# Where a 65 MB zero fill is issued, where the next layer's weights are prepared, and which pools wait tile by tile, in a kernel of a mixture-of-experts layer and a Mamba layer

## The chip, the cores and the metric

The kernel runs on one core of a Trainium2 chip. The metric is the device time of one execution in microseconds (us); lower is better. Times are medians of several executions. One further execution was recorded by the profiler; all durations and positions below are from that one, counted from the start of its span.

## What is computed

The input is an image batch of 32 x 128 channels x 56 x 56, so T = 100352 tokens of 128 channels. Layer 0 is a 7x7 depthwise convolution, a norm over channels, and a mixture of 8 experts with 2 experts per token and a fixed capacity:

```
x = dwconv7x7(input); x = layernorm(x) ; xf = x.reshape(T, C)
topv, topi = top_k(xf @ Wg, 2);  wts = softmax(topv)
order = argsort(-wts[:, 0])              # better tokens get slots first
cap = int(1.25 * T / 8)                  # 15680 slots per expert
slot = expert * cap + position, dropped where position >= cap
buf = zeros(8 * cap, C).at[slot].set(x)  # dispatch
y = gelu(buf @ W1) @ W2                  # per expert
input + x + layer_scale * (sum of y[slot] * gate)
```

Layer 1 works on that result: a 1x1 convolution, then a 3x3 depthwise branch with batch norm and SiLU beside a Mamba branch (norm, projections, causal convolution, a scan over 3136 tokens with 16 states), a 1x1 convolution over both, and a skip connection. Everything is in f32. All biases are inputs, and the weights of both layers are inputs too.

## The kernel before

The work runs in five stages, one after the other. All of it is written in a tile framework: a program (the scheduler) lists the instructions of each engine in an order that it finds by simulating them, taking a later instruction first where an earlier one is not ready, and sets the semaphores. On the chip each engine then works strictly in that order. Only layer 1 fixes its order by hand (`manual_schedule`, in `layer1`).

- **Convolution** (lines 95 to 269): 8 batches b of 4 images. `fill` (L145) loads an image into the single buffer `xt` and PE transposes it into one of two slots; `conv` multiplies 32 groups of 4 channels with banded matrices `toep`. For b = 0 these are built from `raw` windows of `taps_d`, which is written from the first 7 loads of the kernel (L138, L139), and stored to `toep_d`; later batches load them from there (L172). `norm` takes 7 columns of 112 tokens at a time: DVE statistics (L197, L199), ACT scaling to `xa` (L207, three buffers), POOL gain and bias (L210, L211), SP's store to `res_d` (L213), PE transposes and logits (L221, L225). `top2` (L241 on) picks the two experts per token. The last batch's 16 norms have no convolution beside them.
- **Zero fill** (L272 to L274): every slot of `buf_d` that no token takes must hold zeros and, as its token number, T. The 125440 rows of 130 words are written by 14 DMAs from one row `zero` per partition, (k p) order: row k of 112 partitions at a time, 520 bytes per run. They stand after the convolution in the program and wait for nothing but a memset at the start.
- **Routing** (L277 to L442): 24 steps of a bisection for each expert's threshold (each: DVE counts, ACT `sign` sums at L344, PE totals at L323), ranks by scans, and slot numbers turned to 128 partitions. No DMA. DVE is busy most of the time.
- **Dispatch** (L452 to L473): 56 tiles `xg` of 28 x 128 rows, three buffers for each of two picks, loaded by SP from `res_d` (L465), completed by two small DVE copies (L466, L467), and scattered by 1568 indirect DMAs of 128 rows that POOL issues (L469). The scatters write `buf_d`, so they wait for all zero fills.
- **Experts** (L478 to L564): 248 groups of up to 512 rows are loaded from `buf_d` (L552), go through PE, and are added back to `res_d` by 984 indirect DMAs of POOL (L518). The loads wait for all scatters.
- **Layer 1** (L567 on): first the weights are prepared (L570 to L709: some 30 small DMAs, products with gains, transposes), then `layer1` runs 3584 units of a scan in a hand-written order, in which POOL, DVE and ACT each have one step per unit. Its first work is `fetch` (L760, L762), whose `yg` reads `res_d`, and `moe_pe` (L770, L772).

A pool is a region of SBUF; a pool that is opened after another was closed may take the same bytes. As a rule the first instruction that writes such a region waits until everything in the overlapped pools is done. `column` (L89) puts one-word-per-partition vectors into the pool `const`, which stays open throughout, so its loads wait for nothing. All loads and stores except `toep_d<-toep` and the indirect ones are issued by SP, and its DMAs go to the 16 DMA engines in one queue.

Of the kernel before, what the change touches and what calls it, by code (L numbers as in the profile page):

```python
# [13 lines left out]
C = 128  # L14
RW = C + 2
# [7 lines left out]
KF = FF // 128  # L23
GT = 4
# [19 lines left out]
def tile_kernel(tc: tile.TileContext, a: dict, out: bass.AP):  # L44
# [12 lines left out]
    with (  # L57
# [8 lines left out]

        zero = const.tile([TT, 1, RW], F32, name="zero")
        nc.gpsimd.memset(zero, 0.0)
        nc.gpsimd.memset(zero[:, :, C + 1].bitcast(I32), T)
# [26 lines left out]
        routed = tc.tile_pool(name="route", bufs=1)  # L96
# [175 lines left out]
        buf_t = buf_d[: E * CAP].rearrange("(k p) c -> p k c", p=TT)  # L272
        for k in range(0, E * CAP // TT, 80):
            nc.sync.dma_start(out=buf_t[:, k : k + 80, :], in_=zero.to_broadcast([TT, 80, RW]))  # L274


        with (  # L277
            tc.tile_pool(name="rt", bufs=1) as rt,
            tc.tile_pool(name="rs", bufs=2) as rs,
            tc.tile_pool(name="rp", bufs=2, space=PSUM) as rp,  # L280
        ):
            ones_tt = rt.tile([TT, TT], F32, name="ones_tt")
# [161 lines left out]


# [5 lines left out]
        with tc.tile_pool(name="dispc", bufs=1) as dc, tc.tile_pool(name="disp", bufs=3) as dp:  # L451
# [8 lines left out]
            for q in range(QB):  # L460
                for p0 in range(0, TT, XT):
                    for k in range(2):
# [5 lines left out]
                        for j in range(XT):  # L468
                            apart(nc.gpsimd.indirect_dma_start(  # L469
                                out=buf_d[:, :],  # L470
                                out_offset=bass.IndirectOffsetOnAxis(ap=slots[k][:, q, p0 + j : p0 + j + 1], axis=0),
                                in_=xg[:, j, :], in_offset=None,
                            ), "scatter")  # L473

# [3 lines left out]
        with (  # L478
            tc.tile_pool(name="ew", bufs=2) as ew,
            tc.tile_pool(name="eb", bufs=3) as eb,  # L480
# [86 lines left out]
        with (  # L567
            tc.tile_pool(name="w3", bufs=1) as wp,
            tc.tile_pool(name="p3", bufs=2, space=PSUM) as pmm,
        ):  # L570
            def mm_tile(name):
                return pmm.tile([128, 512], F32, name=name, tag="mm")

            def load(v, shape, name, pool=wp):
                t = pool.tile(shape, F32, name=name)
                nc.sync.dma_start(out=t, in_=v)
                return t

            def halves(v, name, pool=wp):
                return load(v.rearrange("(h p) -> p h", p=128), [128, 2], name, pool)  # L580

            cv1t = load(a["cv1_wT"], [C, C], "cv1t")
            cv1b = column(a["L1_conv_cv1_b"], "cv1b")
            def turned(v, t):

                for h in range(2):
                    nc.sync.dma_start(
                        out=t[h * HD : (h + 1) * HD],
                        in_=v[h * 128 : (h + 1) * 128].rearrange("(r d) k -> d r k", r=2),
                    )  # L590

            xpt = wp.tile([128, 2, XR], F32, name="xpt")
            turned(a["x_proj_wT"], xpt)
            dtt = load(a["dt_proj_wT"], [DR, DI], "dtt")
            cvlt = load(a["cv2_wT"][:C, :], [C, C], "cvlt")
            cv2b = column(a["L1_conv_cv2_b"], "cv2b")
            c1b3 = wp.tile([128, 2, 1], F32, name="c1b")
            turned(a["L1_conv_conv1d_b"].unsqueeze(1), c1b3)
            c1b = c1b3[:, :, 0]
            dtb = halves(a["L1_conv_dt_proj_b"], "dtb")  # L600


            aneg = wp.tile([128, 2, DS], F32, name="aneg")
            turned(a["L1_conv_A_log"], aneg)
            nc.scalar.activation(aneg, aneg, AF.Exp)
            nc.vector.tensor_scalar(aneg, aneg, 1e-25, -1.0, ALU.max, ALU.mult)


            bsc = column(a["L1_conv_bn_v"], "bsc")
            bbi = column(a["L1_conv_bn_m"], "bbi")  # L610
            bng = column(a["L1_conv_bn_g"], "bng")
            bnb = column(a["L1_conv_bn_b"], "bnb")
            nc.scalar.activation(bsc, bsc, AF.Sqrt, bias=eps5)
            nc.vector.reciprocal(bsc, bsc)
            nc.vector.tensor_tensor(bsc, bsc, bng, ALU.mult)
            nc.vector.tensor_tensor(bbi, bbi, bsc, ALU.mult)
            nc.vector.tensor_tensor(bbi, bnb, bbi, ALU.subtract)


            bnt = wp.tile([128, 2, 2], F32, name="bnt")  # L620
            for k in range(2):
                for r in range(2):
                    for j, v in enumerate((bbi, bsc)):
                        nc.scalar.copy(bnt[k * HD : (k + 1) * HD, r, j : j + 1], v[r * HD : (r + 1) * HD, :])

            wk = wp.tile([C, DC, DI], F32, name="wk")
            wz = wp.tile([C, DI], F32, name="wz")
            wo = wp.tile([128, 2, C], F32, name="wo")
            dd = wp.tile([128, 2, 128], F32, name="dd")
            dwd = wp.tile([C, 9, C], F32, name="dwd1")  # L630
            cv1c = wp.tile([C, C], F32, name="cv1c")
            cv1cb = wp.tile([C, 1], F32, name="cv1cb")
            zb = wp.tile([128, 2], F32, name="zb")
            early = wp.tile([DC - 1, DI], F32, name="early")
            with tc.tile_pool(name="w3t", bufs=1) as wt:
                dw1 = load(a["L1_conv_dw_w"].rearrange("c o h w -> c (o h w)"), [C, 9], "dw1", wt)
                for t in range(9):
                    nc.vector.tensor_scalar_mul(dwd[:, t, :], ident, dw1[:, t : t + 1])
                dcol = wt.tile([128, 2, 1], F32, name="dcol")
                turned(a["L1_conv_D"].unsqueeze(1), dcol)  # L640
                for h in range(2):
                    nc.vector.tensor_scalar_mul(dd[:, h, :], ident, dcol[:, h, :])


                row = wt.tile([C, 1], F32, name="row")
                nc.vector.tensor_reduce(row, cv1t, AX.X, ALU.add)
                nc.vector.tensor_scalar_mul(row, row, -1.0 / C)
                nc.vector.tensor_scalar(cv1c, cv1t, row, None, ALU.add)
                p = mm_tile("p_mb")
                nc.tensor.matmul(p[:, 0:1], lhsT=mean_w, rhs=cv1b, start=True, stop=True)  # L650
                nc.vector.tensor_tensor(cv1cb, cv1b, p[:, 0:1], ALU.subtract)

                gb = wt.tile([128, 2, C], F32, name="gb")
                nc.sync.dma_start(out=gb[:, 0, :], in_=a["L1_conv_ln_g"].partition_broadcast(128))
                nc.sync.dma_start(out=gb[:, 1, :], in_=a["L1_conv_ln_b"].partition_broadcast(128))
                inp = wt.tile([128, 4, C], F32, name="inp")
                turned(a["L1_conv_in_proj_w"][:DI], inp[:, 0:2, :])
                nc.sync.dma_start(  # L660
                    out=inp[:, 2:4, :], in_=a["L1_conv_in_proj_w"][DI:].rearrange("(h p) c -> p h c", p=128)
                )
                junk = wt.tile([128, 4, C], F32, name="junk")
                wb = wt.tile([128, 4], F32, name="wb")
                nc.vector.tensor_tensor(junk, inp, gb[:, 1:2, :].to_broadcast([128, 4, C]), ALU.mult)
                nc.vector.tensor_reduce(wb, junk, AX.X, ALU.add)
                nc.vector.tensor_tensor(inp, inp, gb[:, 0:1, :].to_broadcast([128, 4, C]), ALU.mult)
                wm = wt.tile([128, 4], F32, name="wm")
                nc.vector.tensor_reduce(wm, inp, AX.X, ALU.add)
                nc.vector.tensor_scalar_mul(wm, wm, 1.0 / C)  # L670
                nc.vector.tensor_tensor(inp, inp, wm.unsqueeze(2).to_broadcast([128, 4, C]), ALU.subtract)
                nc.vector.tensor_copy(zb, wb[:, 2:4])
                c1w = wt.tile([128, 2, DC], F32, name="c1w")
                turned(a["L1_conv_conv1d_w"].rearrange("i o k -> i (o k)"), c1w)

                miss = wt.tile([128, 2, DC], F32, name="miss")
                nc.vector.tensor_tensor(miss, c1w, wb[:, 0:2].unsqueeze(2).to_broadcast([128, 2, DC]), ALU.mult)
                for k in range(1, DC):
                    nc.vector.tensor_tensor(miss[:, :, k], miss[:, :, k], miss[:, :, k - 1], ALU.add)
                nc.vector.tensor_tensor(c1b, c1b, miss[:, :, DC - 1], ALU.add)  # L680
                p = mm_tile("p_ms")
                for h in range(2):

# [524 lines left out]
```

## Time and profile before

| | us |
|---|---|
| median of 3 runs | 16481.53 |
| lowest, highest | 16472.82, 16503.21 |
| the profiled execution | 16440.87 |
| its span | 16439.1 |
| convolution, to the last logits | 0 to 1665 |
| routing | 1665 to 1992 |
| dispatch, first to last scatter | 2002 to 3998 |
| experts, to the last scatter | 4002 to 5927 |
| weights of layer 1, to the first `p_moe` on `yg` | 5929 to 5953 |
| layer 1 | 5953 to 16439 |

The stages are read from the first and last starts of their lines (L229, L441, L469, L518, L772). The profiled execution is 40.7 us below the median of the others. In views that list instructions in order of time, the columns are start, duration, engine, line, operation, output<-input and count, and in brackets the idle time before and what ended it; `SPq` is SP's queue of DMA issues, where the duration is that of the issue, not of the transfer, so a long one is an issue that was held up.

### The profile page before, as it was taken

The numbers are of one execution on the slowest core, as the hardware profiler recorded it, in microseconds if no ns is written. First come the engines' busy times: TensorE is split into PE (matmuls) and PEld (weight loads), VectorE is DVE, ScalarE is ACT, GpSimd is POOL, SyncE is SP. The second block draws the span as 40 slices with busy tenths as digits, with TensorE's granted clock in tenths as the row PEclk, the third lists the DMA queues.
The fourth block names the chain that finished last, engine by engine and source line by source line (L and its number), as shares of the span: only waits on it lengthen the run. The fifth ranks groups of instructions, "written<-read, shape, count | busy, mean of one in ns | idle before, by whom it ended". The sixth has DMA issues, their size and how long they took to land. (4 is left out here: it accounts for less than half of the span.)

```text
span 16439.1 us, 246023 instructions
## 1 busy us (share of the span) xinstructions
PE 12744.6 (78%) x91548; PEld 6997.7 (43%) x91548; DVE 11159.9 (68%) x9974; ACT 10663.7 (65%) x20955; POOL 13614.8 (83%) x9017
## 2 busy tenths in 40 slices
PE   5997200002999989998898999999989899989998
PEld 4997100001777744444444444444444444444443
DVE  1564700000111149999999999999999999999999
ACT  3555300001444458888888888888888888888887
POOL 1434177777888879999999999999999999999999
PEclk8997555556999999999999999999999999999999
DMA  9879233333555545555555555555555555555555
GB/s 257 237 231 230 67 102 106 102 106 76 71 70 72 70 103 175 175 174 176 174 176 174 175 175 176 173 175 177 174 174 173 175 176 174 174 177 175 173 176 162
DMA packets 1360754, 2572.09 MB, mean 156 GB/s; under 512 B 139112, under 2 KB 801856, under 8 KB 1355456
## 3 DMA queue, kind: packets, MB, share of 16 engines
q1 hardware_dynamic: 1163072, 2361.89, 47.6%
q0 software_dynamic: 196480, 194.45, 6.9%
q8 instruction: 721, 11.81, 0.3%
q14 instruction: 481, 3.94, 0.1%
HBM read 2180.38 MB, written 375.43 MB: 155 GB/s over the span
## 5 line engine op out<-in xcount | busy, mean ns | idle before, releaser
L1053 POOL TENSOR_TENSOR db<-du,bb 128x896 f32<-128x896 f32 x3584 | 6856.5, 1938 | 17.6
L1059 ACT ACTIVATE da<-dt,aneg 128x449 f32<-128x449 f32 x7168 | 4577.8, 639 | 269.2 <-DVE prod L1074 86.5
L1068 DVE TENSOR_TENSOR_SCAN da<-da,db 128x898 f32<-128x898 f32 x2240 | 4523.6, 2019 | 1.9 <-ACT da L1059 1.5
L1013 PE MATMUL py<-prod,ident 64*64 64x448 f32 x28672 | 3100.0, 545 | 23.1 <-POOL prod L1074 17.5
L1068 DVE TENSOR_TENSOR_SCAN hs<-da,db 128x898 f32<-128x898 f32 x1344 | 2673.2, 2014 | 469.4 <-ACT db L1080 438.3
L1074 POOL TENSOR_TENSOR prod<-hs,cb 128x896 f32<-128x896 f32 x1344 | 2599.7, 1934 | 432.9 <-PE p_cvc L783 323.1
L1074 DVE TENSOR_TENSOR prod<-da,cb 128x896 f32<-128x896 f32 x2240 | 2446.0, 1092 | 217.3 <-issue 3.6
L560 ACT COPY xc<-ept 128x512 f32<-128x512 f32 (+1 forms) x248 | 144.1, 581 | 2905.2 <-DMA xb<-buf_d 2016.3
L469 POOL DMA_INDIRECT buf_d<-xg,slot x1568 | 1518.0, 968 | 486.2 <-issue 484.7
L518 POOL DMA_INDIRECT res_d<-ys,xb x984 | 1588.8, 1615 | 340.4 <-issue 275.7
L558 PE MATMUL ept<-ident,xb 128*128 128x128 f32 (+1 forms) x984 | 188.7, 274 | 2016.0 <-DMA xb<-buf_d 2016.0
L1013 PEld LDWEIGHTS py<-prod,ident 64*64 64x64 f32 x28672 | 1042.7, 132 | 1448.6 <-issue 1173.6
L868 PE MATMUL p_xm<-te,wk 128*128 128x448 f32 x3584 | 1415.8, 546 | 0.7 <-DVE te L852 0.6
L466 DVE COPY xg<-gate 128x28 f32<-128x28 f32 x56 | 12.1, 233 | 1776.2 <-DMA buf_d<-xg,slot 1776.1
L510 DVE TENSOR_TENSOR ys<-py,b2t 128x512 f32<-128x512 f32 (+2 forms) x256 | 170.8, 670 | 1460.5 <-PE py L504 1447.6
L504 PEld LDWEIGHTS py<-w2t,hh 128*128 128x128 f32 x7872 | 936.3, 191 | 175.7 <-issue 112.9
L504 PE MATMUL py<-w2t,hh 128*128 128x128 f32 x7872 | 985.0, 278 | 0.3
L558 PEld LDWEIGHTS ept<-ident,xb 128*128 128x128 f32 (+1 forms) x984 | 124.5, 143 | 2019.5 <-issue 2019.1
L180 PE MATMUL pc<-xc,toep 112*112 112x112 f32 (+1 forms) x8192 | 933.5, 270 | 49.0 <-ACT toep L169 45.9
L868 PEld LDWEIGHTS p_xm<-te,wk 128*128 128x128 f32 x3584 | 657.7, 189 | 731.4 <-issue 573.4
L210 POOL TENSOR_TENSOR xa<-xa,lng 112x896 f32<-112x896 f32 x128 | 267.5, 2090 | 771.3 <-ACT xa L207 711.9
L180 PEld LDWEIGHTS pc<-xc,toep 112*112 112x112 f32 x8192 | 878.6, 184 | 59.2 <-ACT toep L169 53.7
(244 smaller groups left out, 19714.4 us busy)
## 6 DMA issues: line engine op xcount, KB each, us to landing
bb<-bc_d SPq DMA_DIRECT2D x1792, 448.0 KB
cb<-bc_d SPq DMA_DIRECT2D x1792, 448.0 KB
toep<-toep_d SPq DMA_DIRECT2D x448, 392.0 KB
xg<-res_d SPq DMA_DIRECT2D x56, 1792.0 KB
buf_d<-zero SPq DMA_DIRECT2D x14, 4550.0 KB
xb<-buf_d SPq DMA_DIRECT2D x240, 260.0 KB
xt<-in_x SPq DMA_DIRECT2D x32, 1568.0 KB
res_d<-xa SPq DMA_DIRECT2D x128, 392.0 KB
```

Of the source, the lines that this page charges most:

```text
L180: nc.tensor.matmul(pc[:, c, :, lo:hi], lhsT=tp[c // 2][:, c % 2, 6 - 2 * o : 8 - 2 * o, :], rhs=s4[:, c, :, lo + o - 1 : hi + o - 1], star ...
L210: nc.gpsimd.tensor_tensor(xa, xa, lng.unsqueeze(1).to_broadcast([TT, w, C]), ALU.mult)
L469: apart(nc.gpsimd.indirect_dma_start(out=buf_d[:, :], out_offset=bass.IndirectOffsetOnAxis(ap=slots[k][:, q, p0 + j : p0 + j + 1], axis=0) ...
L504: nc.tensor.matmul(py[:n, j, :], lhsT=hh[:, k, j * 128 : j * 128 + n], rhs=w2t[:, k, :], start=k == 0, stop=k == KF - 1,)
L518: apart(nc.gpsimd.indirect_dma_start(out=res_d[:, :], out_offset=bass.IndirectOffsetOnAxis(ap=xb[:n, j, C + 1 : C + 2].bitcast(I32), axis= ...
L558: nc.tensor.transpose(pt[:, j * 128 : j * 128 + n], xb[:n, j, :C], ident[:n, :n])
L868: nc.tensor.matmul(p[:, :CH1], lhsT=s["wk"][:, k, hs], rhs=d["te"][:, k : k + CH1], start=k == 0, stop=k == DC - 1 and not first,)
L1013: nc.tensor.matmul(ps[r][h * HD : (h + 1) * HD, :CH1], lhsT=lhsT(rs, h), rhs=rhs[rs, h, :], start=start, stop=stop,)
L1053: nc.gpsimd.tensor_tensor(dbv[i][:, :, 1:], st[g]["du"], units[u].pop("bb"), ALU.mult)
L1059: nc.scalar.activation(da[:, h * W1 : (h + 1) * W1], st[g]["dt"][:, h, :], AF.Exp, scale=s["aneg"][:, h, i : i + 1])
L1068: nc.vector.tensor_tensor_scan(hs, da, dbs[i], 0.0, ALU.mult, ALU.add)
L1074: eng.tensor_tensor(w["prod"], w["hs"][:, :, 1:], w.pop("cb"), ALU.mult)
```

## The change

- The tile `zero` is no longer one row in `const`, filled at the start, but 35 rows in each of 128 partitions (18200 bytes) in the routing stage's pool `rt`. Two POOL memsets fill it there, and SP issues 28 fills of 2275 KB. Partition p now owns 980 successive rows of `buf_d` ("(p k) c -> p k c"), so each fill writes 128 runs of 18200 bytes. All 28 are written down ahead of the routing's other work.
- The preparation of layer 1's weights becomes a function `weights`, word for word, and is called in the dispatch after q = 3 of its 7 rounds. The pool `w3` of its results is opened before the dispatch and stays open through the experts; its scratch pool `w3t` and a PSUM pool `p3t` live as long as the dispatch. `layer1` gets the results as a dictionary.
- The pools `rt`, `rs`, `w3t`, `dispc`, `disp`, `ew`, `eb`, `l1`, `l2`, `l3` get `reuse_waits="tile"`: each tile waits only for the earlier tiles whose bytes it takes, and not for whole pools. `w3` does not get it.
- The pool `route` is placed at the other side of SBUF (`side="right"`), so the pools after it start where the convolution's started, just behind `const`.

```diff
-        zero = const.tile([TT, 1, RW], F32, name="zero")
-        nc.gpsimd.memset(zero, 0.0)
-        nc.gpsimd.memset(zero[:, :, C + 1].bitcast(I32), T)
...
-        routed = tc.tile_pool(name="route", bufs=1)
+        routed = tc.tile_pool(name="route", bufs=1, side="right")
...
-        buf_t = buf_d[: E * CAP].rearrange("(k p) c -> p k c", p=TT)
-        for k in range(0, E * CAP // TT, 80):
-            nc.sync.dma_start(out=buf_t[:, k : k + 80, :], in_=zero.to_broadcast([TT, 80, RW]))
         with (
-            tc.tile_pool(name="rt", bufs=1) as rt,
-            tc.tile_pool(name="rs", bufs=2) as rs,
+            tc.tile_pool(name="rt", bufs=1, reuse_waits="tile") as rt,
+            tc.tile_pool(name="rs", bufs=2, reuse_waits="tile") as rs,
             tc.tile_pool(name="rp", bufs=2, space=PSUM) as rp,
         ):
+            zero = rt.tile([128, ZT, RW], F32, name="zero")
+            nc.gpsimd.memset(zero, 0.0)
+            nc.gpsimd.memset(zero[:, :, C + 1].bitcast(I32), T)
+            buf_t = buf_d[: E * CAP].rearrange("(p k) c -> p k c", p=128)
+            for k in range(0, E * CAP // 128, ZT):
+                nc.sync.dma_start(out=buf_t[:, k : k + ZT, :], in_=zero)
...
+        def weights(wp, wt, pw):
...
+        w3pool = tc.tile_pool(name="w3", bufs=1)
+        w3p = w3pool.__enter__()
...
+            tc.tile_pool(name="w3t", bufs=1, reuse_waits="tile") as w3t,
+            tc.tile_pool(name="p3t", bufs=2, space=PSUM) as p3t,
+            tc.tile_pool(name="dispc", bufs=1, reuse_waits="tile") as dc,
+            tc.tile_pool(name="disp", bufs=3, reuse_waits="tile") as dp,
...
+                if q == QB // 2:
+                    w3 = weights(w3p, w3t, p3t)
...
-            layer1(locals())
+            layer1(w3 | locals())
```

## The prediction

> **What bounds the kernel now.** I read the engine slices of the page first, then SP's issues at both ends of the convolution, then the waits there, then the seams between the stages.
>
> ```profile
> PE   5997200002999989998898999999989899989998
> POOL 1434177777888879999999999999999999999999
> PEclk8997555556999999999999999999999999999999
> DMA  9879233333555545555555555555555555555555
> ```
>
> A slice is 411 us. The last 26 (layer 1) are full on POOL and PE, slices 10 to 13 (experts) on PE, and 5 to 8 (dispatch) hold only POOL's 1568 scatters, about one per 1.27 us. The change takes no instruction out of these three stages. So it can only act on the convolution (slices 0 to 3), the routing (4) and the seams. The DMA row is highest where the zero fill runs: in slices 0 and 3.
>
> SP's issues in order of time show what the fill does at the start:
>
> ```profile
> 3.13 0.43 SPq L274 DMA_DIRECT2D buf_d<-zero  x1
> 3.96 23.57 SPq L138 DMA_DIRECT2D xt<-in_L_conv_dw_kernel  x7
> 29.75 0.34 SPq L274 DMA_DIRECT2D buf_d<-zero  x1
> 31.39 18.48 SPq L139 DMA_DIRECT2D taps_d<-xt  x1
> 49.92 0.43 SPq L274 DMA_DIRECT2D buf_d<-zero  x1
> 57.87 18.18 SPq L145 DMA_DIRECT2D xt<-in_x  x1
> 76.08 4.60 SPq L162 DMA_DIRECT2D raw<-taps_d  x6
> 96.27 0.36 SPq L145 DMA_DIRECT2D xt<-in_x  x1
> ```
>
> The scheduler had put fills into SP's gaps. Each is 4.66 MB and holds up the small transfer behind it for about 18 us: taps, store, first image, in a chain on which the first convolution depends. Two more fills follow at 114.9 and 140.5, and the first `pc` matmul starts at 159.55. The DMA's own speed with these 520 byte runs is read from windows in which the fills are alone or nearly so: 195 GB/s (15 to 20 us), at worst 177 (20 to 25), with the engines' busy share above 1. One fill is at 1334; the remaining 8 are in the convolution's tail. There ACT waits for a buffer of `xa` that stands in the queue behind a fill (waits, 1490 to 1670 us):
>
> ```profile
> POOL xa L210 <- ACT xa L207: 113.1, 12, 38.6
> ACT xa L207 <- DMA res_d<-xa: 23.2, 5, 5.7
> ```
>
> **The change part by part.** All gains and losses are of the span, 16439.1 us.
>
> *Start.* Without fills the 7 tap loads are issued by 3.96 + 7 x 0.45 = 7; the gap from the last tap load's issue to the store was 3.9 us, so the store goes at 11; it has landed 8 us later at most (49.9 to 57.9, a fill behind it): 14 to 19. Then four images through the one buffer: undisturbed, they were 15.9 and 14.4 us apart (96.27, 112.14, 126.55), and from the last load's landing to the first `pc` there were 7 us. 17 + 4 x 15.4 = 79, against 159.55: **80 us**. The `raw` loads lie in the gaps as they did. What comes after is not changed: batch 0 goes on at 302 GB/s (159 to 337 us), paced as before. Bounds: 60 if the 16 first `raw` loads now collide with the images, 95 with the fill that was still draining until 175. The fill at 1334 held one `toep` load for 16.7 us, but PE's weight loads waited 2.8 us in all for such loads after 411 us: nothing.
>
> *Tail.* 16 norms take 142.6 us from the first `p_xa` (1522.57) to the last logits. The five waits are 23 us. In the stretch with no wait, `p_xa` starts are 7.0 us apart (1522.57, 1529.56, 1536.5): 15 x 7.0 + 4.9 = 110 would be 33 less. I take **30**; bounds 10 (the ring of three buffers waits for undisturbed stores too) and 55 (ACT alone, 3.9 + 1.0 + 0.3 per norm).
>
> *Fill.* It now starts after the last norm: `zero` takes the first bytes of the convolution's pool, where the logit weights and the gains lie. The memset is 4550 words on POOL; that of `xt` was 3248 in 2.81, so 4 us, hidden beside DVE. SP and the DMA engines are idle from 1700 to 1990, and routing needs neither. No row here shows 18 KB runs into DRAM. Bounds: 65.2 MB at 320 GB/s (the fastest window of mixed loads, 115 to 125 us) are 204 us; at the 177 of the slowest 520 byte window 368. Routing lasts 327. I take a value towards the fast end, 230, since the run grows 35-fold: hidden. Without that cover, 368 + 6 means the fill ends 47 us past routing's end. At 200 GB/s, 326, it would end on time within 6 us.
>
> The Trainium skill ("DMA: Bandwidth & Descriptors", Specifications) has line rate reached from 512 bytes on, which speaks against this edit: 520 byte runs would be as good as 18 KB. By that the fill takes 326 us, ends as routing ends, and the gain of the next paragraph is lost. The same page (Rules for kernel authors) wants transfers issued early and waited for late; the start above, 80 us lost to early fills in one queue, goes against it here.
>
> *Head of the dispatch.* Loads of `xg` waited for the whole routing (1992.26), and the first scatter came at 2002. Tile by tile, the first `xg` needs only the bytes of the keys, whose last use is some 40 us before routing's end, and its slots are there at 1981.3. If the load is early, the first scatter comes between 1982 and 1995: **12**. Bounds: 20, and -45 if the fill is late (47, with the load that then queues behind it, less what tile waits still save).
>
> *Weights in the dispatch.* Some 60 DVE instructions (under 20 us), 10 on ACT, 20 on PE, engines that are idle there: DVE is busy 15 of 1995 us. In SP's queue the some 25 loads (5929 to 5943: 14 us of issue) stand among `xg` loads that are up to six tiles of 28 x 1.27 = 36 us ahead. Behind a DVE instruction that waits for a weight stand the copies of the next tile, and POOL waits for those. The first seven `xg` issues take 47 us, so a load behind them costs nothing unless more than one tile's copies stand behind it. I take nothing; at worst one tile, 36, within the -45 above.
>
> *Head of the experts.* `xb` waits for the scatters in any case, but five small loads stood before it (3999.2 to 4002.0): **3**, bounds 0 and 6.
>
> *Head of layer 1.*
>
> ```profile
> 5929.52 0.35 SPq L576 DMA_DIRECT2D cv1t<-in_cv_wT  x1
> ...
> 5942.36 0.43 SPq L576 DMA_DIRECT2D wop<-in_L_conv_out_proj_w  x1
> 5942.83 0.43 SPq L762 DMA_DIRECT2D yg<-res_d  x1
> ```
>
> The last scatter has landed at 5928.7. Then SP issues the weights, and only behind them `yg`; PE multiplies it at 5953.02, after the transposes of the weights. Afterwards `yg` is SP's first issue, at 5929.5. A 256 KB load took 4.0 us from issue to use (`w2t`, 4000.35 to 4004.33), so PE starts at 5933.5: **19**, bounds 15 and 22. The hand-written order behind it is the same: no cover hides it, and what is late next is that chain itself.
>
> *Sum.* 80 + 30 + 12 + 3 + 19 = 144: span 16295. The profiled execution is 40.7 us below the median, so I take the difference off the median: 16481.5 - 144 = **16337.5**.
>
> **Rivals.**
>
> *A load behind the fill stops ACT: slower.* In ACT's order of before stands an instruction of layer 1's weights in the middle of the routing:
>
> ```profile
> 1674.57 22.33 SPq L89 DMA_DIRECT2D cv1b<-in_L_conv_cv_b  x1
> 1697.51 0.45 SPq L89 DMA_DIRECT2D bsc<-in_L_conv_bn_v  x1
> ```
> ```profile
> 1703.57 0.29 ACT L613 ACTIVATE bsc<-bsc,eps 128x1 f32<-128x1 f32 x1 [24.97 <-DMA bsc<-in_L_conv_bn_v]
> 1704.26 1.04 ACT L344 ACTIVATE sign<-key,odd 112x896 f32<-112x896 f32 x1 [0.40 <-DVE key L316]
> ```
>
> SP issued the columns behind the last fill, ACT's square root of `bsc` waited 25 us for one, and the first `sign` stood behind it. That was free, since the keys came at 1704. If the columns again go behind the fill, and now behind all of it, they land 210 to 332 us after the last logits (6 + 204 or 326); the keys need 39 us in any case, so the bisection starts 171 to 293 us late. With the other gains that is 27 to 149 slower: 16509 to 16631, some 16570. It decides as soon as the fill takes over 177 us with the columns behind it. Against it: the columns wait for nothing, and the gaps in SP's order at 3 to 140 us, which fills took, now go to the next ready instruction, which the columns are. One in ten.
>
> *The fill is the bound at the dispatch.* At 177 GB/s, 144 - 12 - 45 = 87: 16394. For it: runs of 520 bytes already keep the engines busy. Against it: nothing else runs on them.
>
> *The start is bound by bytes, not by the chain,* or the gaps are filled by something else: 144 - 80 = 64: 16417.5. For it: slices 0's DMA share of 0.97. Against it: a third of slice 0's first 76 us is one issue held up after another, with PE at nothing. Both of the last two: 144 - 80 - 57 = 7, 16474, no change.
>
> **How the numbers follow.** Forecast 0.72, fill late 0.10, no gain at the start 0.05, both 0.03, ACT stopped 0.10. A measurement here tells 0.2% (33 us) from no change, so faster 0.87, same 0.03, slower 0.10. The forecast's own ends are 95 + 55 + 20 + 6 + 22 = 198 and 60 + 10 - 10 + 0 + 15 = 75: 16283 to 16406. To take in the late fill and the lost start I go to 16425; the slower rival and the double loss, 0.13, stay outside.
>
> **What would show it.** Right: no `buf_d<-zero` before the last logits, the first `pc` near 79, the last logits near 1555, fills of 28 over in less than 320 us after it, first scatter within 325 us of the last logits, `yg` within 2 us of the last landing of `res_d`. Wrong: a square root or another instruction of the weights that waits among the `sign` sums; a first scatter that a fill releases; a scatter spacing other than 1.27 us; or a layer 1 whose length is not 10486 us (16439 - 5953), which nothing here should alter.

## The result, and the profile after

| us | before | after |
|---|---|---|
| median | 16486.53 (4 runs, 16472.82 to 16503.21) | 16311.94 (4 runs, 16301.03 to 16320.97) |
| the profiled execution | 16440.87 | 16320.97 |
| its span | 16439.1 | 16319.2 |

The ratio is 0.9893, 95% interval 0.9876 to 0.9911: faster by 174.6 us between the medians, where 144 was forecast (a median of 16337.5). The two profiled spans differ by only 119.9. The marks of the two traces say why, with the gain so far in the last column:

| mark, start of the instruction | before | after | gained |
|---|---|---|---|
| first `pc` | 159.6 | 69.9 | 89.7 |
| last `pc` | 1501.1 | 1392.1 | 109.0 |
| last logits | 1664.9 | 1537.1 | 127.8 |
| last slot | 1991.8 | 1862.5 | 129.3 |
| first scatter | 2002.1 | 1873.2 | 128.9 |
| last scatter | 3996.8 | 3866.3 | 130.5 |
| first transpose of the experts | 4007.5 | 3871.9 | 135.6 |
| last add to `res_d` | 5925.6 | 5790.0 | 135.6 |
| first `p_moe` on `yg` | 5953.0 | 5795.9 | 157.1 |
| end of the span | 16439.1 | 16319.2 | 119.9 |

Ahead of layer 1 the gain is 157.1. Layer 1 then took 10523 us instead of 10486; the experiments below show that 10486 was peculiar to that one execution of before.

First the engine slices of the page of after, one digit per 408 us:

```profile
PE   7995200005999989998999889999989898999988
POOL 2443377777888889999999999999999999999999
PEclk9996555557999999999999999999999999999999
DMA  8785333333555545555555555555555555555555
```

PE is at 7 tenths in slice 0 instead of 5, and the DMA row falls from 9 to 8 there and from 9 to 5 in slice 3, although the fill now runs at the end of slice 3 and the start of 4. Dispatch, experts and layer 1 look the same.

SP's issues at the start of after, in order of time:

```profile
3.78 3.19 SPq L135 DMA_DIRECT2D xt<-in_L_conv_dw_kernel  x7
7.01 0.43 SPq L86 DMA_DIRECT2D cv2b<-in_L_conv_cv_b  x1
7.49 0.43 SPq L86 DMA_DIRECT2D bsc<-in_L_conv_bn_v  x1
...
9.05 0.33 SPq L136 DMA_DIRECT2D taps_d<-xt  x1
...
11.77 0.33 SPq L142 DMA_DIRECT2D xt<-in_x  x1
12.14 3.24 SPq L159 DMA_DIRECT2D raw<-taps_d  x6
25.57 0.36 SPq L142 DMA_DIRECT2D xt<-in_x  x1
...
41.91 0.36 SPq L142 DMA_DIRECT2D xt<-in_x  x1
...
56.60 13.18 SPq L142 DMA_DIRECT2D xt<-in_x  x2
```

The seven tap loads take 3.2 us instead of 23.6, the store follows at 9 instead of 31, and the first four images are loaded at 11.8, 25.6, 41.9 and 56.6, that is 13.8 to 16.3 apart. The gaps went to layer 1's columns (L86). So ScalarE's square root of `bsc`, the instruction of the slower rival, has its column within the first 10 us (ScalarE of after in order of time):

```profile
9.72 1.28 ACT L487 ACT_TABLE_LOAD   x1 [9.72 <-DMA bsc<-in_L_conv_bn_v]
11.02 0.29 ACT L487 ACTIVATE bsc<-bsc,eps 128x1 f32<-128x1 f32 x1
```

In the convolution's tail SP holds nothing but stores, one after the other, and then the fill (the second view ends at 1560 us, so it has 10 of the 28):

```profile
1413.52 119.39 SPq L210 DMA_DIRECT2D res_d<-xa  x16
1542.53 12.68 SPq L280 DMA_DIRECT2D buf_d<-zero  x10
```

The waits of after there, 1390 to 1540 us (who waited for whom, us in total, times, longest):

```profile
POOL xa L207 <- ACT xa L204: 94.3, 16, 38.6
ACT xa L204 <- POOL xa L208: 28.4, 7, 4.2
```

ScalarE no longer waits for a store of `xa`, but 28 us appear that are put down to GpSimd. The fill itself, in windows (stretch, its length, busy time of PE, PEld, DVE, ACT and POOL, then granted clock, DMA share, GB/s):

```profile
1545.00:1600.00 55.00, 1.54 (x6) 1.35 (x6) 52.21 (x73) 14.95 (x26) 0.00 (x0) 0.50 1.00 427
1600.00:1655.00 55.00, 4.62 (x18) 4.03 (x18) 47.00 (x117) 39.83 (x75) 0.00 (x0) 0.50 1.00 426
...
1697.00:1750.00 53.00, 17.76 (x44) 8.87 (x44) 44.38 (x81) 25.54 (x46) 0.00 (x0) 0.63 0.00 1
```

427 GB/s: the 65.2 MB are out at 1697, 155 us after the first issue and 165 us before routing ends. The two other seams, SP's and POOL's first, then PE's, in order of time:

```profile
1862.59 0.33 SPq L450 DMA_DIRECT2D cv1t<-in_cv_wT  x1
1862.97 83.33 SPq L614 DMA_DIRECT2D xg<-res_d  x8
```
```profile
1873.16 1.10 POOL L618 DMA_INDIRECT buf_d<-xg,slot  x1 [47.99 <-issue]
1874.56 0.99 POOL L618 DMA_INDIRECT buf_d<-xg,slot  x1 [0.30 <-issue]
1875.85 0.97 POOL L618 DMA_INDIRECT buf_d<-xg,slot  x1 [0.30 <-issue]
```
```profile
5793.02 0.33 SPq L776 DMA_DIRECT2D yg<-res_d  x1
```
```profile
5795.92 2.05 PE L786 MATMUL p_moe<-perm,yg 112*128 112x112 f32 x8 [23.27 <-DMA yg<-res_d]
```

At layer 1 `yg` is SP's first issue, as argued. At the dispatch it is not `xg` that stands first but `cv1t`, a weight of layer 1, and it was issued when routing's last slot was done; the first scatter comes 10.7 us after that slot, against 10.3 before.

### The profile page after: what moved, and what is told of

Its sections match the earlier page's. It is cut to its first block, busy times and chain, and to the rows that moved or that the text cites. A ratio compares the mean times of both kernels' runs of the same rounds, so it can differ in the third digit from the quotient of the medians.

```text
span 16319.2 us, 246039 instructions
## 1 busy us (share of the span) xinstructions
PE 12773.7 (78%) x91548; PEld 7020.1 (43%) x91548; DVE 11158.6 (68%) x9974; ACT 10652.4 (65%) x20952; POOL 13610.8 (83%) x9017
## 5 line engine op out<-in xcount | busy, mean ns | idle before, releaser
L904 PE MATMUL p_z<-te,wz 128*128 128x448 f32 x896 | 539.6, 738 | 466.9 <-ACT xm L898 466.9
```

The source lines that it names most:

```text
L904: nc.tensor.matmul(p[:, :CH1], lhsT=s["wz"][:, h * 128 : (h + 1) * 128], rhs=d["te"][:, DC - 1 :], start=True, stop=True,)
```

## The experiments

The dispatch has one of two lengths from execution to execution: 1993 to 1998 us (before and after above, and the runs `x9_both` and `x10_after`) or 2169 to 2173 (the others). The median scatter takes 0.97 us in both. In the longer dispatches 103 to 107 of the 1568 scatters, from some 280 us or more behind the first one on, take 1.7 to 1.9 us, which makes the mean 1.05, and some 90 gaps between scatters are over 0.5 us instead of 0.3. Why was not traced. Both lengths occur with the kernel before and with the changed one. So totals are compared only at one pace, and else marks ahead of the first scatter and distances between marks. The runs were on several chips; each is compared with runs of before on its own chip.

**Is layer 1 longer?** The kernel before, unchanged, once more.

> The kernel before, unchanged, profiled once more. In the two profiled executions layer 1 (from the first p_moe on yg to the end) took 10486 us before and 10523 after. Theory: this is a spread between executions, since the one profiled before was 32 to 62 us below its other runs; then layer 1 takes between 10500 and 10540 us here, and all marks up to 5953 us come again within 2 us. Rival: the change itself made layer 1 longer by 37 us; then it takes 10486 here again, within 5.

16696.68 us; ratio to the other runs of before on that chip 1.0001 (0.9991 to 1.0011). From the first `p_moe` on `yg` to the end it took 10512 us; all later runs, of whatever variant, took 10507 to 10522. So 10486 was the odd one, and the change does not touch layer 1. Against my expectation the earlier marks did not come again within 2 us: the last logits were at 1708 instead of 1665. The fill with its 520 byte runs was slower in this execution (180 GB/s from 5 to 25 us, 203 in the first one). So what the change gains can differ by chip.

**The position of the fill.** Filled early as before, but with long runs: 14 rows per partition (7280 bytes) in the convolution's pool `wp`, and the fills written down behind the convolution, outside routing.

```diff
-ZT = 35
+ZT = 14
+            zero = wp.tile([128, ZT, RW], F32, name="zero")
...
+            for k in range(0, E * CAP // 128, ZT):
+                nc.sync.dma_start(out=buf_t[:, k : k + ZT, :], in_=zero)
...
-            zero = rt.tile([128, ZT, RW], F32, name="zero")
```

> The changed kernel, but the zero tile lies in the convolution's pool (14 rows, 7280 byte runs, 70 fills), so that fills are free to go into SP's gaps at the start and into the tail again. Theory (position and price of a fill both count: what a fill holds up is its own time in the queue, and with long runs that is 1.86 MB at 427 GB/s = 4.4 us instead of 23): about 7 fills go early, the first pc comes at 85 to 105 instead of 70, the last logits 20 to 40 later than after the change, time some 16330 to 16355. Rival 1 (position alone counts): first pc at 150 or later, 16400 or more. Rival 2 (run length alone counts): first pc at 70 to 75, 16300 to 16320.

16582.72 us; 0.9931 of before (0.9914 to 0.9947), 106 us faster. The first `pc` came at 76.0, 6 us later than in after, and the last logits at 1537.6, like after's. But a fill is now 0.93 MB (not 1.86, as I had reckoned), and only 7 of them, 6.5 MB, stood ahead of the first `pc`, where before had 5 with 23.3 MB. So the 6 us against 90 are not the price of the same bytes: it is some 0.9 us per MB against 3.9, from smaller fills as well as longer runs, and this run does not tell the two apart. When the last fills are alone in the queue, 1560 to 1608 us, their 7280 byte runs go at 417 GB/s. The loss came elsewhere, in routing, which took 404 us instead of 325 (waits, 1535 to 1960 us):

```profile
DVE ones_tt L282 <- DMA buf_d<-zero: 77.7, 1, 77.7
```

Routing's first tile takes bytes of `zero`, and the last fills were still reading them. I had not expected that.

**The length of the runs.** The fill where the change puts it, with the old pattern.

```diff
-            zero = rt.tile([128, ZT, RW], F32, name="zero")
+            zero = rt.tile([TT, 1, RW], F32, name="zero")
...
-                nc.sync.dma_start(out=buf_t[:, k : k + ZT, :], in_=zero)
+                nc.sync.dma_start(out=buf_t[:, k : k + 80, :], in_=zero.to_broadcast([TT, 80, RW]))
```

> The changed kernel, but filled with one row per partition and 520 byte runs as before, 14 fills, still in the routing stage. Theory (the run length sets the rate): 65.2 MB at about 195 GB/s are 335 us from 1541 on, so the fill ends near 1876, past the end of routing at 1862; the first scatter comes 8 to 20 us later than after the change (1881 to 1893), time 16320 to 16335. Rival (the fill is fast because it is alone in the queue, whatever its runs): the DMA moves over 400 GB/s from 1545 on, the fill ends near 1700, and the first scatter stays at 1873.

16569.65 us; 0.9922 of before (0.9905 to 0.9938). The windows, with the columns as above:

```profile
1545.00:1600.00 55.00, 1.74 (x6) 1.34 (x6) 52.88 (x74) 11.01 (x19) 0.00 (x0) 0.50 1.25 172
1600.00:1655.00 55.00, 4.60 (x18) 4.01 (x18) 47.07 (x115) 40.29 (x77) 0.00 (x0) 0.50 1.29 163
```

The same bytes take 395 us, more than the 335 that I had expected; the last fill lands at 1937, 68 us after the last slot, and the first scatter comes at 1948.6, 80 after that slot instead of 11. So the new form of the fill is worth about 69 us here, and this is the second rival, made by hand. The convolution keeps its gain: the first `pc` at 68.9, the last logits at 1541.5. So the position alone, with the old runs, makes the start and the tail faster, and the new form keeps the fill from being late. The edit also brings back 112 partitions instead of 128, one row that is read 80 times, and neighbouring rows from different partitions. That the length of the run is what counts, and not one of these, was not tried by itself.

**The weights.** Their preparation and the pool `w3` back behind the experts, all else as in after.

```diff
-                if q == QB // 2:
-                    w3 = weights(w3p, w3t, p3t)
...
+            with tc.tile_pool(name="w3t", bufs=1) as w3t:
+                w3 = weights(w3p, w3t, pmm)
```

> The changed kernel, but the weights of layer 1 are prepared behind the experts again. Theory: yg is again behind the weights in SP's queue, so the first p_moe on yg comes 21 us later after the last landing of the experts' scatters (24 instead of 3 us). And the load cv1t, whose pool w3 waits for all of the routing's pools, no longer stands ahead of the first xg load in SP's queue, so the first scatter comes 6 to 10 us earlier after the last slot (1 to 5 us instead of 10.7). Net 11 to 15 us slower in the marks, 16320 to 16330. Rival on the second point: the xg loads wait for the routing's end themselves; then the first scatter stays 10.7 us after the last slot and the net is 21.

16514.72 us; 0.9887 of before (0.9871 to 0.9904). From the last add to the first `p_moe` on `yg` 27.3 us, like before's 27.4, where after has 5.9: 21.4 for the move. And, as the expectation had it but not the prediction, the first scatter came 1.2 us after the last slot instead of 10.7. The totals agree with the marks: `x3_fill_520`, on the same chip and at the same pace, is 55 us slower than this run, and its late fill (69) less what the weights lose here (21.4 less 9.5 at the first scatter) would be 57.

**The control**, the changed kernel with the three that follow:

> The changed kernel itself, once more, so that the other three have it on the same chip. Theory: the marks up to the first p_moe come as in its first profile, and its time is 1.0 to 1.1% below the kernel before, with layer 1 as long as in the kernel before within the spread between executions (20 us). Rival: the dispatch or layer 1 differs by more than that from the kernel before on the same chip.

16498.06 us; the ratio to before there, 0.9953 (0.9910 to 0.9995), mixes two groups of runs of before, 9 at 16435 to 16460 and 22 at 16627 to 16659, while the ten of after are at 16484 to 16515. I take the upper group for the one at after's pace there, since the groups are about as far apart as the two lengths of the dispatch; against it the change gains 147. That is an inference from the totals, as no run of before on this chip has a trace. On this chip 9 of 31 runs of before had the lower total and none of the 40 runs of the changed kernel and the three that follow; on the other chips every kernel kept one pace, by its totals. So it isn't shown that the change leaves the pace alone, and against all 31 runs of before the gain is 0.5%.

**What holds the first scatter.** One word: the pool of the prepared weights waits tile by tile, too.

```diff
-        w3pool = tc.tile_pool(name="w3", bufs=1)
+        w3pool = tc.tile_pool(name="w3", bufs=1, reuse_waits="tile")
```

> The changed kernel with reuse_waits=tile for the pool w3 too. Theory (the first load of the weights, cv1t, stood ahead of the first xg load in SP's queue and waited for the whole routing): cv1t now waits only for the bytes of the zero tile, the xg loads come before the last slot, the first scatter follows the last slot by 1 to 3 us instead of 10.7, and the time is 8 to 10 us below the changed kernel. Rival (something else at the head, the copies or the iota): 10.7 again and no difference.

16496.99 us (0.9967 of before, 0.9923 to 1.0010), no different from the control. But SP's issues are:

```profile
1697.35 0.33 SPq L450 DMA_DIRECT2D cv1t<-in_cv_wT  x1
1821.94 64.41 SPq L614 DMA_DIRECT2D xg<-res_d  x6
```

`cv1t` goes when the fill is over, `xg` 39 us before the last slot, as the forecast had it, and the first scatter 2.0 us after that slot. The total does not show these 9 us, and why is open. In the two traces the control's convolution was 8.6 us shorter, so that both first scatters came at 1863, and its experts were 8 us shorter; that does not explain why the medians of ten runs each are only 1 us apart.

**The slower rival, made by hand.** Column and root of `bsc`, taken out of `weights`, stand behind the fills, and the sums of the bisection behind the root.

```diff
+            with tc.issue_after(filled.ins):
+                bsc = column(a["L1_conv_bn_v"], "bsc")
+            with tc.issue_after(expd.ins):
+                root = nc.scalar.activation(bsc, bsc, AF.Sqrt, bias=eps5)
...
+                with tc.issue_after(root.ins):
+                    count(cand, ALU.is_ge, 1.0)
```

> The slower rival of the prediction, made by hand: the load of bsc is put behind the 28 fills in SP's queue, its square root behind the Exp of the routing on ACT, and the bisection's sums behind the square root. Theory: the load lands when the fills are through, about 160 us after the last logits; the first sign comes then instead of 39 us after them, the routing takes 325 + 120 = 445 us, and the time is 110 to 130 us above the changed kernel, still below the kernel before, since the fill (155 us) is shorter than the 177 from which the rival would decide. Rival: the small load overtakes the fills on the 16 engines; then the routing takes less than 345.

16619.35 us; 1.0011 of before (0.9971 to 1.0051) with its two groups mixed. That is 121 above the control and still 26 below the upper group of before. The wait is the one that was priced (waits, 1540 to 1700 us):

```profile
ACT bsc L309 <- DMA bsc<-in_L_conv_bn_v: 147.6, 1, 147.6
```

Routing takes 440 us instead of 325. It ends up not slower than before, as the fill takes 155 us and not the 177 from which I had let it decide.

**The pools.** All ten pools of the change wait as whole pools again, each by the same edit.

```diff
-            tc.tile_pool(name="rt", bufs=1, reuse_waits="tile") as rt,
+            tc.tile_pool(name="rt", bufs=1) as rt,
...
```

> The changed kernel without any reuse_waits=tile, so that every pool waits for whole pools. Theory (tile by tile waits are worth little here, since what binds at the seams are data, not bytes): last logits as before; routing at most 5 us longer; the first scatter 10 to 12 us after the last slot; from the last scatter to the first transpose of the experts 8 to 11 us instead of 5.6; from the last add to the first p_moe on yg 5 to 10 instead of 5.9; in all 5 to 15 us above the changed kernel. Rival: they are a good part of the gain, 30 us or more.

16502.32 us (0.9932, 0.9900 to 0.9964), 4 above the control, which isn't told from nothing. Routing 325.6, last slot to first scatter 10.8, last scatter to experts 6.7 instead of 5.6, layer 1's head 5.9. As the change stands, waiting tile by tile brings it next to nothing: the one pool without it stands first in the queue. What `side="right"` does by itself was not tried.

**Both repairs that I had in mind**, `w3` tile by tile, and four buffers for `xa` and `raw`, which share them, beside the changed kernel on one chip.

```diff
-                        raw = cp.tile([TT, 2, 8, TS], F32, name="raw", tag="xa", bufs=3)
+                        raw = cp.tile([TT, 2, 8, TS], F32, name="raw", tag="xa", bufs=4)
...
-                xa = cp.tile([TT, 2 * 8 * TS], F32, name="xa", bufs=3)[...]
+                xa = cp.tile([TT, 2 * 8 * TS], F32, name="xa", bufs=4)[...]
...
-        w3pool = tc.tile_pool(name="w3", bufs=1)
+        w3pool = tc.tile_pool(name="w3", bufs=1, reuse_waits="tile")
```

> The changed kernel with two edits: `w3` waits tile by tile as well, and the buffers `xa` and `raw` of the start number four instead of three. Theory (the ring of three sets the tail's pace, and one load at the head of SP's queue sets the dispatch's start): from the last `pc` to the last logits some 10 to 18 us less than the changed kernel's 145, `p_xa` 7 us apart without the alternation of 6.95 and 9.07, and the first scatter 2 us after the last slot instead of 10.7; together 18 to 27 us below the changed kernel of the same call. Rival (the written order of the adds on ScalarE and the moments sets the tail, and the buffers only follow it): the tail stays within 3 us of the changed kernel's, and the total goes down by 9 us at most.

> The changed kernel as the control of the run beside it: the first `pc` at 68 to 71 us, last slot to first scatter 10 to 11 us, last `back` to the first product of layer 1 5 to 6 us, and layer 1 10510 to 10525 us from its first product to the end.

16332.62 us (0.9891 of before, 0.9875 to 0.9908) against 16318.53 (0.9882, 0.9865 to 0.9898) for the control. Here the two are at one pace, and with both repairs the kernel is 14 us slower. My theory of the tail fell: from the last `pc` to the last logits both have 145 us, and with four buffers the wait for GpSimd is still there, over the tail 28.4 us in 7, as in after. The first scatter again comes 2.0 us after the last slot instead of 10.8, so from the last slot on 9 us are gained. The convolution took more than that away: with the extra buffer the scheduler wrote another order, the last images of the batches are loaded 170.6 us apart instead of 165.6, and the last `pc` is 22 us later.

**What sets the tail, then?** In the trace of after, VectorE's and GpSimd's instructions around one of these waits (two queries, in order of time):

```profile
1457.20 0.26 DVE L199 RECIPROCAL rs<-rs 112x7 f32<-112x7 f32 x2
1457.43 2.12 DVE L201 SCALAR_TENSOR_TENSOR nm<-mv,rs 112x7 f32<-112x7 f32 x2
1459.51 1.04 DVE L196 BATCH_NORM_AGGREGATE mv<-st 112x2 f32<-112x6 f32 x14
```
```profile
1457.38 2.07 POOL L208 TENSOR_TENSOR xa<-xa,lnb 112x896 f32<-112x896 f32 x1
```
```profile
1459.56 2.81 ACT L204 ACTIVATE xa<-xc,nm,rs 112x128 f32<-112x128 f32 x5 [4.02 <-POOL xa L208]
```

`nm`, 7 words per partition, is busy for up to 2.06 us (148 ns at the least) and ends when GpSimd's addition ends, at 1459.5; then ScalarE, which needs `nm`, goes on. The profile names GpSimd, for it ended last. To try that, `nm` of the last batch column by column, with `rs` as a scalar instead of a second tile:

```diff
-                nc.vector.scalar_tensor_tensor(nm, mv[:, :, 0], -1.0, rs, ALU.mult, ALU.mult)
+                    for j in range(w):
+                        nc.vector.tensor_scalar(nm[:, j : j + 1], mv[:, j, 0:1], rs[:, j : j + 1], -1.0, ALU.mult, ALU.mult)
```

> The changed kernel, with `nm` of the last batch computed column by column: 7 instructions of one word per partition with `rs` as their scalar, instead of one instruction that reads the two tiles `mv` and `rs`. Theory (a VectorE instruction with two inputs in SBUF is held until GpSimd's running instruction ends, so `nm` of 7 words takes up to 2.06 us, and ScalarE's next `xa` waits for it): the 7 instructions take under 0.2 us each whatever GpSimd does, ScalarE's 4 us waits in the tail go, `p_xa` come 7 us apart without the 9.07, and from the last `pc` to the last logits it is 130 to 136 us instead of 145; 9 to 15 us in all. Rival (the written order holds `nm` back, or GpSimd itself is late): the alternation of 6.95 and 9.07 stays, and the tail with it, within 3 us. An end between: if an instruction with a scalar from SBUF is held as well, each `nm` still ends with GpSimd's instruction.

16489.89 us (0.9882 of before, 0.9866 to 0.9899). The control was not run beside it, but from the last `pc` to the last logits it is 145.0 to 145.2 us in the changed kernel and in every other variant, on four chips. The answer on `nm` (duration ns min, median, max):

```profile
L205 DVE TENSOR_SCALAR nm<-mv,rs x112: 192/204/215, 1406.1 to 1511.1; 112x1 f32<-112x1 f32 x112
```
```profile
1464.46 2.08 POOL L212 TENSOR_TENSOR xa<-xa,lnb 112x896 f32<-112x896 f32 x1
1464.50 1.79 DVE L205 TENSOR_SCALAR nm<-mv,rs 112x1 f32<-112x1 f32 x14
```

They run right through GpSimd's addition, at 0.2 us each. `p_xa` are 6.95 and 8.05 us apart by turns instead of 6.95 and 9.07, and from the last `pc` to the last logits it is 138.0 instead of 145.1. So the hold is real and is worth 7 us; I had expected 9 to 15. The Trainium skill ("GPSIMD Engine Reference", Specifications) has GpSimd's SBUF interfaces shared with VectorE, with contention for VectorE instructions with two SBUF inputs; the runs agree, 2.06 us with two and 0.2 with one. ScalarE still waits 2.2 us every other time, and the spacing stays 1.1 us over 6.95 then. In the same trace VectorE is idle for 3.7 us, until 1464.14, before it adds a bias to `lg`, for which it waits for PE's `p_lg`; in its order `rs` and `nm` stand behind that. So the written order, which was the rival, seems to hold `nm` back for the rest; no run tried it.

## Why the prediction was right, and where its steps were not

The forecast held, 25.6 us above the median. By marks ahead of layer 1 it was 144 for 157.1. That the sum came so close is in part luck: convolution up to the last `pc` brought 29 more than its 80, tail and head of the dispatch together 22 less than their 42, and these errors cancel. At one pace on each chip the change gained 175 here, 192 in `x10_after`, and 147 in `x5_after`.

- **Start, 80: measured 90 at the first `pc`, 97 to 102 at the image loads of the later batches.** The mechanism was right. The rivals speak of a third of the first 76 us in issues held up one after another; the three are 60 of them. The chain was mis-sized by 9 us, 69.9 instead of 79: the first image goes at 11.8, not 17, and the four steps from there take 14.5 us each, not 15.4. The other 7 to 12 I put down to the fill that was still draining until 175, which I had only as a bound; no run tried this alone.
- **The fill at 1334, "nothing": about 8.** From the last load of an image to the last `pc` it was 177.2 us before and 169.6 after. I had gone by PE's waits for `toep` loads; PE had no `pc` matmul from 1346 to 1372, while the `toep` load that stood behind the fill was held up until 1356, and the waits named other releasers. That the fill is the cause is read from this one trace. With the start that is 109 at the last `pc`.
- **Tail, 30: measured 19.** The waits for stores are gone, as argued. But I took 7.0 us as the spacing of all `p_xa`, from the undisturbed first three; it is 6.95 and 9.07 by turns. I had looked for the limit in the ring of buffers; four buffers changed nothing there, and 7 us of it are VectorE held by GpSimd.
- **Fill hidden, 230 us, bounds 204 to 368: right in kind, faster than my fast bound.** It took 155 us. The bound came from a window of mixed loads with shorter runs and was no bound for 18 KB runs. The skill's line rate from 512 bytes on ("DMA: Bandwidth & Descriptors", Specifications) does not hold here: 163 to 172 GB/s with 520 bytes, 427 with 18200.
- **Head of the dispatch, 12: nothing. This step failed.** I put `xg` early because its own pool waits tile by tile. But SP's queue is in order, and the load before it, `cv1t`, goes into the pool that I had noted as the one without tile waits. I priced the loads of the weights among later `xg`, and never asked which stands first. The first scatter came 336 us after the last logits, where 325 was to be the sign of being right. With that pool mended, or the weights elsewhere, it came 2.0 and 1.2 us after the last slot: 9 of the 12 were there to be had at this mark, though no total shows them.
- **Weights in the dispatch, nothing: right for their own cost.** The scatters' spacing stayed at 1.27 us, and the dispatch took 1993 us against 1995; what they cost is at the head, above.
- **Head of the experts, 3: 5. Head of layer 1, 19: 21.5**, confirmed by putting the weights back.
- **Layer 1, 10486, "which nothing here should alter": not altered**, but that number was one execution's; the others have 10507 to 10523, after too. The medians differ by 30.6 more than the forecast's 144: 13.1 of it is in the marks, and 17.5 lies between the profiled executions and the medians and was not traced.
- **Rivals.** The load behind the fill did not come about, for the reason given against it; made by hand, its price was 115 us in routing. Its point of decision, 177 us, agrees with that run, which with a fill of 155 us is still 26 below before. The late fill came about only with the old runs.

## What to carry to other kernels

A large transfer from small runs costs twice, as a slow transfer and as a queue that holds every small one behind it. Moving it away from a chain of small transfers brought the convolution's gain even with the old runs; its new form, with long runs, made it short enough to hide in its new place. Where a wait is relaxed for one pool, look at the first instruction that each in-order queue issues behind it: one load for a pool that still waits as a whole gives the gain back. And a wait on an engine's end may be a third engine's hold: look for an instruction far longer than its shortest.

## What the runs showed of the hardware

- Stores of 18200 byte runs from SBUF to DRAM went at 427 GB/s with the DMA engines at a share of 1.00; runs of 520 bytes at 163 to 172 in `x3_fill_520` (177 to 195 at the start of before) at shares of 1.25 to 1.29; runs of 7280 bytes at 417 to 419 (`x2_fill_early`).
- A scatter of 128 rows took 0.97 us in the median of every execution, with 0.3 us between two. In the longer dispatches a fifteenth of them took 1.7 to 1.9 us.
- A VectorE instruction with two SBUF inputs of 7 words took 0.15 us, and up to 2.06 while GpSimd ran an addition over 896; with one input and a scalar it took 0.2 per word throughout.
